# Where the feed-forward's rounded numbers become bfloat16: on VectorE, or on GpSimd behind the rounding products

## The chip, the core and the metric

The kernel runs on one core of a Trainium2 chip. A core has TensorE (PE: matrix products, written to PSUM), VectorE (DVE), ScalarE (ACT), GpSimd (POOL) and SyncE (SP), which here issues nearly all the DMA transfers. Each engine works through its own queue in order, and the engines wait for one another by semaphores. The metric is device microseconds (us) of one execution, the median of the runs. Lower is better.

## The reference, cut to what matters

The work is one decoder layer for 32 images of 256 tokens with 256 features: self-attention (16 query heads, 4 key heads), windowed cross-attention to a context (16 heads, window 64), and a gated feed-forward with 1024 inner features. Each is followed by a residual and a layer norm. The feed-forward rounds its activations to whole numbers, once ahead of the gate and up products and once ahead of the down product:

```python
def _act_quant(x):
    scale = 127.0 / jnp.clip(jnp.max(jnp.abs(x), axis=-1, keepdims=True), 1e-05)
    xq = jnp.clip(jnp.round(x * scale), -128.0, 127.0) / scale
    return x + jax.lax.stop_gradient(xq - x)

def _bitlinear(x, w):
    return jnp.einsum('bsi,oi->bso', _act_quant(x), _weight_quant(w))

gate = jax.nn.silu(_bitlinear(x, w_gate))
up = _bitlinear(x, w_up)
return _bitlinear(gate * up, w_down)
```

The rounded values are whole numbers up to 127, which bfloat16 holds exactly, so these three products run in bfloat16. All other products are float32.

## The kernel before, in words

An image's 256 tokens are two tiles of 128 partitions. The images are pipelined: while image b is in its self-attention, image b-1 is in its cross-attention and image b-2 in its feed-forward, and the projections of image b+1 are made ahead. Time is cut into slots, 16 to an image. Each part of an image is a Python generator (`self_inputs`, `cross_inputs`, `self_output`, `cross_output`, `feed_forward`) that is started in a given slot; a `yield n` in it puts what follows n slots later. The order of PE, DVE and ACT is the order in which the program is written, slot by slot. The order of POOL and of SP's queue is decided by the scheduler, from the order of the program and what each instruction waits for.

The steps that the change and the prediction touch:

- Self-attention. `project` (line 330) makes keys and queries in PSUM; DVE multiplies them with the rotary tables into `psin` and `qT` or `kT` (lines 339 and 346); `turned` (line 312) issues four DMA copies that swap the halves of psin into `other`; POOL adds that to qT or kT (line 354). Scores `s` (line 393) go through DVE (line 409, with the bias and the row's extreme) and ACT's exponential (line 427), are transposed on PE (line 471), copied by ACT (line 480) and multiplied with the values (`o`, line 492). The reciprocal sums are spread by DVE (`wide`, line 443), a DMA transpose (`planes`, line 448) and a POOL copy (`R`, line 455), and DVE multiplies o with R into `oT` (line 505). `wo` (line 513) is the output product; behind it stand the residual and statistics (lines 523, 177, 178, 528 to 531), the normalised `row` on DVE (line 538), its transposes `zqT` (line 204), and the query product `xq` of the cross-attention (line 550).
- Cross-attention. `cross_inputs` makes keys and values from the context: key statistics `rstd_zc` on POOL (lines 184 to 186), the normalised context on ACT (line 198), its transposes `zcT`, the products `xk` (line 622) and `xv` (line 634). The keys are biased on ACT (line 568), copied by two DMAs with neighbours swapped (line 573), rotated on POOL (lines 584 to 586), and copied by eight DMAs into `kTz` (line 658), one buffer for all images. The values go to `xvaug` (line 642), parts of which two DMAs copy (lines 649 and 650). `xs` (line 674) are the scores: four products at once, each on 32 rows of kTz. DVE's line 688 and ACT's line 704 follow, then transposes `xt` (line 713), ACT's copy `xpT` (line 715), and the product with the values, `xo` (line 729).
- Feed-forward. DVE finds the row's largest value and the factors (lines 790 to 799). POOL makes the rounding product (line 803): value times factor plus the constant MAGIC = 12582912 in float32, after which the sum's low bits hold the whole number. Subtracting MAGIC gives the number, written as bfloat16 into `xib` (line 805). Two DMA transposes turn xib into `xiT` (line 809), which is the stationary operand of gate and up (`ff`, line 816). After ACT's tanh (line 830) and DVE's products (lines 831 and 837), the same is done per tile with 1024 columns: largest value (line 843), factors (lines 845 to 850), POOL's rounding product (line 852), the subtraction into `hib` (line 855), a DMA transpose into `hiT` (line 857), the down product `ffo` (line 863), and residual and statistics (lines 867, 177, 178). `out_dram` is written by SP (line 194), and the next image's transposed tokens `xT` are loaded by SP (line 111).

In the kernel before, both subtractions are DVE instructions, written one slot behind the POOL product that they need.

Of the kernel before, what the change touches and what calls it, by code (L numbers as in the profile page):

```python
# [10 lines left out]
BF16 = mybir.dt.bfloat16  # L11
# [3 lines left out]
ALU = mybir.AluOpType  # L15
AX = mybir.AxisListType

P = 128
L = 256
NT = L // P  # L20
# [14 lines left out]
INNER = 1024  # L35
# [3 lines left out]
MAGIC = 12582912.0  # L39
# [12 lines left out]
def kernel(  # L52
# [27 lines left out]
    nc = tc.nc  # L80
# [5 lines left out]
    def ctile(shape, dtype, name):  # L86
        return const.tile(shape, dtype, name=name, tag=name)
# [3 lines left out]
    def bank(name, shape=(P, 512), dtype=F32):  # L91
        return ps.tile(list(shape), dtype, tag="b", name=name)
# [10 lines left out]
    def work(name, shape, bufs=2, dtype=F32):  # L103
        return sb.tile(list(shape), dtype, tag=name, name=name, bufs=bufs)

    def small(name, n):
        return sb.tile([P, 8], F32, tag="small", name=name, bufs=48)[:, 0:n]
# [47 lines left out]
    for i in range(2):  # L155


        t = ctile([P, (NT + 1) * XH * XE + 32 - XE], F32, f"xvaug{i}")
# [14 lines left out]
    def stats(src, name):  # L173

        st = small("st", 6)
        mv = small(f"mv_{name}", 2)
        nc.vector.bn_stats(st, src)
        nc.vector.bn_aggr(mv, st)
        return mv

    def rstd_of(mv, name):

        rb = small(f"rstd_{name}", 2)
        nc.gpsimd.tensor_scalar(rb[:, 0:1], mv[:, 1:2], EPS, None, ALU.add)
        nc.gpsimd.tensor_tensor(rb[:, 0:1], rb[:, 0:1], neg_half[:, 0:1], ALU.pow)
        nc.gpsimd.tensor_scalar(rb[:, 1:2], mv[:, 0:1], rb[:, 0:1], -1.0, ALU.mult, ALU.mult)
        return rb
# [598 lines left out]
    def feed_forward(b):  # L786
        x2 = state[b]["x2"]

        s = small("ffs", NT)
        nc.vector.tensor_reduce(s, x2, AX.X, ALU.max, apply_absolute_value=True)  # L790
        nc.vector.tensor_scalar(s, s, QUANT_MIN, None, ALU.max)
        up = small("ffup", NT)
        nc.vector.reciprocal(up, s)
        nc.vector.tensor_scalar(up, up, 127.0, None, ALU.mult)
        g_of = small("ffg", NT)
        nc.vector.tensor_scalar(g_of, s, ff_scale["gate"], 0.5, ALU.mult, ALU.mult)
        u_of = small("ffu", NT)
        nc.vector.tensor_scalar(u_of, s, ff_scale["up"], None, ALU.mult)
        nc.vector.tensor_tensor(u_of, u_of, g_of, ALU.mult)
        xi = work("tr", [P, NT, D], 3)  # L800
        xib = work("xib", [P, NT, D], 1, BF16)
        for t in range(NT):
            nc.gpsimd.tensor_scalar(xi[:, t, :], x2[:, t, :], up[:, t : t + 1], MAGIC, ALU.mult, ALU.add)
        yield
        nc.vector.tensor_scalar(xib, xi, MAGIC, None, ALU.subtract)  # L805

        xiT = work("xiT", [P, NT, NDC, P], 1, BF16)
        for t in range(NT):
            nc.sync.dma_start_transpose(xiT[:, t, :, :], xib[:, t, :])
        yield 3  # L810
        gu = work("gu", [P, NT, INNER], 1)

        def hidden(name, t, half):
            pg = bank("ff")
            for dc in range(NDC):
                nc.tensor.matmul(  # L816
                    pg,
                    xiT[:, t, dc, :],
                    ff_w[name][:, dc, half * 512 : (half + 1) * 512],
                    start=(dc == 0),  # L820
                    stop=(dc == NDC - 1),
                )
            return pg


        for t in range(NT):
            for half in range(2):
                pg = hidden("gate", t, half)
                cols = gu[:, t, half * 512 : (half + 1) * 512]
                nc.scalar.activation(cols, pg, AF.Tanh, scale=g_of[:, t : t + 1])  # L830
                nc.vector.scalar_tensor_tensor(cols, cols, 1.0, pg, ALU.add, ALU.mult)  # L831
            yield 1 if t == 0 else 3
        for t in range(NT):
            for half in range(2):
                pg = hidden("up", t, half)
                cols = gu[:, t, half * 512 : (half + 1) * 512]
                nc.vector.tensor_tensor(cols, cols, pg, ALU.mult)
            yield 1 + t
        d_ofs, hiTs = [], []
        for t in range(NT):  # L840

            m = small("ffm", 1)
            nc.vector.tensor_reduce(m, gu[:, t, :], AX.X, ALU.max, apply_absolute_value=True)
            sh = small("ffsh", 1)
            nc.vector.tensor_scalar(sh, m, u_of[:, t : t + 1], QUANT_MIN, ALU.mult, ALU.max)
            hup = small("ffhup", 1)
            nc.vector.reciprocal(hup, sh)
            nc.vector.tensor_scalar(hup, hup, u_of[:, t : t + 1], 127.0, ALU.mult, ALU.mult)
            d_of = small("ffd", 1)
            nc.vector.tensor_scalar(d_of, sh, ff_scale["down"], None, ALU.mult)  # L850
            d_ofs.append(d_of)
            nc.gpsimd.tensor_scalar(gu[:, t, :], gu[:, t, :], hup, MAGIC, ALU.mult, ALU.add)
            yield
            hib = work("hib", [P, INNER], 2, BF16)
            nc.vector.tensor_scalar(hib, gu[:, t, :], MAGIC, None, ALU.subtract)
            hiT = work("hiT", [P, NIC, P], 2, BF16)
            nc.sync.dma_start_transpose(hiT, hib)
            hiTs.append(hiT)
        yield 2
        for t in range(NT):  # L860
            py = bank("ffo")
            for ic in range(NIC):
                nc.tensor.matmul(  # L863
                    py[:, 0:D], hiTs[t][:, ic, :], ff_w["down"][:, ic, :], start=(ic == 0), stop=(ic == NIC - 1)
                )
            y = x2[:, t, :]
            nc.vector.scalar_tensor_tensor(y, py[:, 0:D], d_ofs[t], y, ALU.mult, ALU.add)
            mv = stats(y, "y")
            rstd = rstd_of(mv, "y")
            yield  # L870
            last.append(partial(scaled, y, y, rstd))
        last.append(partial(nc.sync.dma_start, out[b].rearrange("(t p) d -> p t d", p=P), x2))
        del state[b]
# [16 lines left out]
    for b in range(B):  # L890
        s0 = 16 * b
        if b:
            at(s0 - 15, self_inputs(b))
        at(s0 + 2, cross_inputs(b))
        for t in range(NT):
            at(s0 + 9 + 8 * t, self_output(b, t))
            at(s0 + 4 * CROSS + 11 + 8 * t, cross_output(b, t))
        at(s0 + 4 * CROSS + 26, feed_forward(b))
# [154 lines left out]
```

## Time and profile before

| | |
|---|---|
| median of 3 runs | 2186.22 us (2183.72 to 2188.77) |
| span of the profiled execution, first to last instruction | 2184.1 us |
| time of that execution beside its span | none is recorded; its span lies 2.1 us under the median |
| busy: PE | 2096.9 us (96%) |
| busy: DVE | 1778.0 us (81%) |
| busy: ACT | 1600.0 us (73%) |
| busy: POOL | 1285.1 us (59%) |
| mean granted PE clock | 0.983 |
| DMA | 177.57 MB, mean 81 GB/s |

The profile is one execution. Busy time is the time in which an engine has an instruction in work; matrix products are pipelined and their ends are modelled. A row of the groups gives line, engine, operation, the tiles written and read, shapes and count, then the busy time in us and the mean of one in ns, then the idle time of the engine just ahead of these instructions and what ended it. A row of the timeline gives start and length in us, engine, line, operation and tiles; what stands in brackets is the idle time ahead of it and its releaser. "SPq" rows are SP issuing DMAs; the transfer lands later.

### The profile page before, as it was taken

The numbers are of one execution on the slowest core, as the hardware profiler recorded it, in microseconds if no ns is written. First come the engines' busy times: TensorE is split into PE (matmuls) and PEld (weight loads), VectorE is DVE, ScalarE is ACT, GpSimd is POOL, SyncE is SP. The second block draws the span as 40 slices with busy tenths as digits, with TensorE's granted clock in tenths as the row PEclk, the third lists the DMA queues.
The fourth block names the chain that finished last, engine by engine and source line by source line (L and its number), as shares of the span: only waits on it lengthen the run. The fifth ranks groups of instructions, "written<-read, shape, count | busy, mean of one in ns | idle before, by whom it ended". The sixth has DMA issues, their size and how long they took to land.

```text
span 2184.1 us, 54367 instructions
## 1 busy us (share of the span) xinstructions
PE 2096.9 (96%) x17316; PEld 1606.7 (74%) x17316; DVE 1778.0 (81%) x6949; ACT 1600.0 (73%) x4833; POOL 1285.1 (59%) x1977
## 2 busy tenths in 40 slices
PE   7899999999999999999999999999999999999983
PEld 5677777777777777777777777777777777777751
DVE  4777888888888888888888888888888888888765
ACT  2478778777778877777877777877777877777862
POOL 4555665566655656655656655656666566666542
PEclk9899999999999999999999999999999999999986
DMA  7432333333333334334334333333343333333211
GB/s 219 111 75 72 82 75 83 77 79 86 89 72 78 83 71 91 86 71 86 76 76 89 82 77 79 78 81 83 86 82 76 81 82 74 90 81 69 53 42 32
DMA packets 326589, 177.57 MB, mean 81 GB/s; under 512 B 242976, under 2 KB 296096, under 8 KB 326304
## 3 DMA queue, kind: packets, MB, share of 16 engines
q1 hardware_dynamic: 324608, 170.52, 34.6%
q8 instruction: 139, 2.28, 0.5%
q10 hardware_dynamic: 1696, 3.57, 0.5%
q14 instruction: 146, 1.20, 0.2%
HBM read 39.50 MB, written 8.39 MB: 22 GB/s over the span
## 4 chain that ended last, share of the span: by engine, by line
PE 74%; DVE 11%; ACT 5%; POOL 4%; DMA 4%; issue 1%; SPq 0%; ACTq 0%; POOLq 0%; DVEq 0%
PE wo L513 10%; PE o L492 8%; PE proj L330 8%; PE t L471 8%; PE s L393 8%; PE ff L816 5%; PE xt L713 4%; PE xo L729 3%; PE xq L550 3%; PE xs L674 3%; PE ffo L863 3%; PE xk L622 3%; DVE p L409 2%; PE xw L775 2%; PE v L362 2%; DVE xib L805 2%
## 5 line engine op out<-in xcount | busy, mean ns | idle before, releaser
L427 ACT ACTIVATE p<-p,nm 128x256 f32<-128x256 f32 x1024 | 511.6, 512 | 197.7 <-DVE nm L409 197.7
L409 DVE CUSTOM_DVE_ANT_0 p<-s,alibi 128x256 f32<-128x256 f32 x1024 | 364.6, 416 | 6.3 <-PE s L393 6.3
L480 ACT COPY pT<-t 128x512 f32<-128x512 f32 x512 | 276.1, 601 | 89.6 <-PE t L471 89.3
L704 ACT ACTIVATE xp<-xp,xnm 128x128 f32<-128x128 f32 x1024 | 331.8, 416 | 0.0
L688 DVE CUSTOM_DVE_ANT_0 xp<-xs,mask 128x128 f32<-128x128 f32 x1024 | 225.9, 285 | 68.1 <-PE xs L674 68.1
L455 POOL COPY R<-planes 128x1024 uint16<-128x1024 uint16 x128 | 175.4, 1370 | 176.3 <-DMA planes<-wide 164.6
L471 PE MATMUL t<-ident,p 128*128 128x128 f32 x2048 | 266.4, 273 | 0.9 <-ACT p L427 0.9
L492 PE MATMUL o<-pT,v 128*64 128x256 f32 x2048 | 260.8, 386 | 1.3 <-ACT pT L480 1.1
L393 PE MATMUL s<-kT,qT 64*128 64x256 f32 x2048 | 255.7, 389 | 0.0
L513 PE MATMUL wo<-wo_sb,oT 128*128 128x256 f32 x1024 | 248.0, 386 | 0.4 <-ACT xpT L715 0.3
L354 POOL TENSOR_TENSOR qT<-qT,other 128x512 f32<-128x512 f32 x128 | 169.4, 1323 | 127.6 <-DMA other<-psin 66.4
L330 PE MATMUL proj<-xT,wq_sb 128*128 128x256 f32 x1024 | 243.1, 381 | 0.0
L471 PEld LDWEIGHTS t<-ident,p 128*128 128x128 f32 x2048 | 234.2, 141 | 9.4 <-ACT p L427 2.6
L393 PEld LDWEIGHTS s<-kT,qT 64*128 64x128 f32 x2048 | 187.3, 186 | 63.4 <-issue 14.3
L492 PEld LDWEIGHTS o<-pT,v 128*64 128x64 f32 x2048 | 143.9, 136 | 104.4 <-issue 21.2
L513 PEld LDWEIGHTS wo<-wo_sb,oT 128*128 128x128 f32 x1024 | 194.9, 193 | 30.9 <-ACT xpT L715 1.1
L427 ACT ACTIVATION_READ_ACCUMULATOR p<-p,nm 128x1 f32 x1024 | 208.0, 203 | 0.0
L330 PEld LDWEIGHTS proj<-xT,wq_sb 128*128 128x128 f32 x1024 | 185.8, 191 | 21.1 <-issue 0.4
L831 DVE SCALAR_TENSOR_TENSOR gu<-gu,ff 128x512 f32<-128x512 f32 x128 | 82.6, 684 | 84.5 <-ACT gu L830 84.3
L713 PEld LDWEIGHTS xt<-ident,xp 128*128 128x128 f32 x1024 | 110.6, 141 | 53.7 <-issue 38.5
L713 PE MATMUL xt<-ident,xp 128*128 128x128 f32 x1024 | 143.3, 281 | 2.1 <-ACT xp L704 2.0
L339 DVE TENSOR_TENSOR psin<-proj,rs_sb 128x512 f32<-128x512 f32 x160 | 109.8, 686 | 38.2 <-PE proj L330 34.6
(146 smaller groups left out, 4325.7 us busy)
## 6 DMA issues: line engine op xcount, KB each, us to landing
other<-psin SPq DMA_DIRECT2D x640, 64.0 KB, 2.0
xT<-in_xt_dram SPq DMA_DIRECT2D x32, 256.0 KB, 2.8
xs<-in_x_dram SPq DMA_DIRECT2D x32, 256.0 KB, 2.8
cs<-in_ctx_dram SPq DMA_DIRECT2D x32, 256.0 KB, 2.8
other<-qb SPq DMA_DIRECT2D x64, 128.0 KB, 2.1
kTz<-tr SPq DMA_DIRECT2D x256, 32.0 KB, 2.0
other<-qb SPq DMA_DIRECT2D x128, 64.0 KB, 2.0
out_dram<-x SPq DMA_DIRECT2D x32, 256.0 KB, 2.3
```

The lines of the kernel that those rows point to most:

```text
L330: nc.tensor.matmul(pq[:, c * L : (c + 1) * L], w[:, dc, c * P : (c + 1) * P], xT[:, dc, :], start=(dc == 0), stop=(dc == NDC - 1),)
L393: nc.tensor.matmul(banks[half][:, rr * L : (rr + 1) * L], qT[rows_, rr, qc * P : (qc + 1) * P], kT[rows_, kc, :], start=(rr == 0), stop=(r ...
L409: nc.vector.tensor_tensor_reduce(p[:, cols], banks[half][:, cols], alibi[:, 2 * (4 * kc + 2 * rp + rr) + half, :], -0.125, 3.0e38, ALU.add ...
L427: nc.scalar.activation(p[:, cols], p[:, cols], AF.Exp, bias=nm[:, rr : rr + 1], scale=-1.0, accum_out=s["sums", i // 2][:, e : e + 1],)
L455: nc.gpsimd.tensor_copy(R.bitcast(U16).rearrange("p (n z) -> p z n", z=2), s.pop(("planes", m)).rearrange("p z r q -> p z (r q)"),)
L471: nc.tensor.transpose(pt[:, j * P : (j + 1) * P], p[half][:, rr * L + kk * P : rr * L + (kk + 1) * P], ident,)
L480: nc.scalar.copy(pT, pt)
L492: nc.tensor.matmul(po[half * HD : (half + 1) * HD, rp * L : (rp + 1) * L], s["v"][:, kk, (2 * kc + half) * HD : (2 * kc + half + 1) * HD], ...
L513: nc.tensor.matmul(py[:, 0:D], s["oT", qc, kc][:, r, :], wo_sb[:, 4 * kc + r, :], start=(kc == 0 and r == 0), stop=(kc == 1 and r == 3),)
L688: nc.vector.tensor_tensor_reduce(p[:, cols], banks[2 * half + j // 2][:, j % 2 * P : (j % 2 + 1) * P], s["mask"][:, qc, :], -1.0, 3.0e38, ...
L704: nc.scalar.activation(p[:, cols], p[:, cols], AF.Exp, bias=s["xnm", i][half][:, j : j + 1], scale=-1.0)
L713: nc.tensor.transpose(pt[:, j * P : (j + 1) * P], p[:, j * P : (j + 1) * P], ident)
```

## The change

The two subtractions of MAGIC move from DVE to POOL, each behind its rounding product and ahead of the `yield`. The first one becomes two instructions of 256 columns in place of one of 512. Nothing else is written differently.

```diff
         for t in range(NT):
             nc.gpsimd.tensor_scalar(xi[:, t, :], x2[:, t, :], up[:, t : t + 1], MAGIC, ALU.mult, ALU.add)
+        for t in range(NT):
+            nc.gpsimd.tensor_scalar(xib[:, t, :], xi[:, t, :], MAGIC, None, ALU.subtract)
         yield
-        nc.vector.tensor_scalar(xib, xi, MAGIC, None, ALU.subtract)
 
         xiT = work("xiT", [P, NT, NDC, P], 1, BF16)
...
             nc.gpsimd.tensor_scalar(gu[:, t, :], gu[:, t, :], hup, MAGIC, ALU.mult, ALU.add)
+            hib = work("hib", [P, INNER], 2, BF16)
+            nc.gpsimd.tensor_scalar(hib, gu[:, t, :], MAGIC, None, ALU.subtract)
             yield
-            hib = work("hib", [P, INNER], 2, BF16)
-            nc.vector.tensor_scalar(hib, gu[:, t, :], MAGIC, None, ALU.subtract)
             hiT = work("hiT", [P, NIC, P], 2, BF16)
             nc.sync.dma_start_transpose(hiT, hib)
```

## The prediction

> **What bounds the kernel now.** I read the page's busy shares and its chain first. About 0.2% is what a measurement of this kernel can tell from no change; that is 4.4 us.
>
> ```profile
> PE 2096.9 (96%) x17316; PEld 1606.7 (74%) x17316; DVE 1778.0 (81%) x6949; ACT 1600.0 (73%) x4833; POOL 1285.1 (59%) x1977
> ...
> PE 74%; DVE 11%; ACT 5%; POOL 4%; DMA 4%; issue 1%; SPq 0%; ACTq 0%; POOLq 0%; DVEq 0%
> ```
>
> TensorE is the bound: in the stretch view PE is busy 1783.9 of the 1800 us from 130 to 1930, in steady state, where an image takes some 64.7 us. Freeing DVE is worth only the little that PE waits for DVE. Next, the groups of DVE and of POOL with shapes kept apart: the two moved conversions, and the POOL rows nearest to their new form.
>
> ```profile
> L855 DVE TENSOR_SCALAR hib<-gu 128x1024 bf16<-128x1024 f32 x64 | 58.1, 908 | 8.9 <-POOL gu L852 8.9
> ...
> L805 DVE TENSOR_SCALAR xib<-tr 128x512 bf16<-128x512 f32 x32 | 44.3, 1384 | 8.3 <-POOL tr L803 7.5
> ```
>
> ```profile
> L852 POOL TENSOR_SCALAR gu<-gu,ffhup 128x1024 f32<-128x1024 f32 x64 | 71.7, 1120 | 79.2 <-DVE ffhup L848 79.0
> ...
> L803 POOL TENSOR_SCALAR tr<-x,ffup 128x256 f32<-128x256 f32 x64 | 29.9, 480 | 0.0
> ...
> L603 POOL CAST ck_i<-ck_i 128x256 f32<-128x256 int32 x32 | 13.2, 412 | 99.1 <-DMA ck_i<-in_cell_k_dram 99.1
> ...
> L224 POOL TENSOR_SCALAR xkv_w<-tr,vecs_sb 128x256 f32<-128x256 f32 x4 | 3.7, 932 | 12.0 <-DMA tr<-in_wxk_dram 11.6 <-DMA tr<-in_wxv_dram 0.3
> ```
>
> Then the timeline around one xib in mid-run (others repeat it).
>
> ```profile
> 975.65 0.93 POOL L803 TENSOR_SCALAR tr<-x,ffup 128x256 f32<-128x256 f32 x2
> ...
> 976.61 1.49 DVE L805 TENSOR_SCALAR xib<-tr 128x512 bf16<-128x512 f32 x1 [0.42 <-POOL tr L803]
> ...
> 979.06 0.51 ACT L427 ACTIVATE p<-p,nm 128x256 f32<-128x256 f32 x1 [3.69 <-DVE nm L409]
> ...
> 980.48 0.41 PE L204 MATMUL zqT<-ident,row 128*128 128x128 f32 x2 [0.25 <-DVE row L538]
> ...
> 983.63 0.91 PE L729 MATMUL xo<-xpT,xvaug 128*32 128x64 f32 x32 [0.39 <-ACT xpT L715]
> ```
>
> Here is the one place in an image where DVE holds up PE: DVE waits 0.42 for POOL, is busy 1.49 with xib, starts its scores late, ACT its exponentials, and PE waits 0.25 and 0.39; that xo run takes 0.91 where other xo runs of 32 take 0.65. Last, SP's queue after it, and PE's first matmuls of the next image's cross-attention.
>
> ```profile
> 974.71 3.41 SPq L312 DMA_DIRECT2D other<-psin  x4
> 978.21 0.54 SPq L649 DMA_DIRECT2D xvaug<-xvaug  x1
> 978.85 0.54 SPq L650 DMA_DIRECT2D xvaug<-xvaug  x1
> 979.48 2.49 SPq L809 DMA_TRANSPOSE xiT<-xib  x2
> 982.07 0.54 SPq L194 DMA_DIRECT2D out_dram<-x  x1
> 982.70 0.41 SPq L111 DMA_DIRECT2D xT<-in_xt_dram  x1
> 983.41 2.47 SPq L312 DMA_DIRECT2D other<-psin  x4
> ...
> 989.32 5.58 SPq L658 DMA_DIRECT2D kTz<-tr  x7
> ```
>
> ```profile
> 997.34 0.50 PE L674 MATMUL xs<-kTz,xqT 32*128 32x256 f32 x4
> ```
>
> SP issues without a pause from 974.7 to 994.9, and at its end stand the kTz copies, which xs at 997.34 needs. The last kTz copy is issued at 994.3 and the page gives 2.0 us from issue to landing: 996.3, 1.05 before xs. Read so in 26 images, it lands 0.04 to 1.92 us before xs, on average 0.98. This margin decides the forecast.
>
> **The change part by part.** In the instruction order of the changed program against that of before, PE, ACT and the rest of DVE keep their order. On DVE 96 instructions go. On POOL each conversion comes behind its rounding product. On SP the xiT transposes move ahead of the projection's four psin copies and the two xvaug copies; the first hiT transpose moves ahead of one planes transpose and one of a pair of query copies.
>
> *xib off DVE.* 32 x 1.38 = 44 us of DVE time, and its wait. DVE would go from its xvaug additions (end 976.2) straight on instead of at 978.0, so some 1.8 us earlier; the scores it needs start on PE at 975.33. ACT follows by the same, and PE's waits go: 0.25 + 0.39 + (0.91 - 0.65) = 0.9 per image. The value matmuls at 991.47 take 2.33 against 1.88 to 1.95 elsewhere, behind an ACT queue that has no gap since 979: up to 0.38 more. So 0.9 to 1.3 per image, over 29 images 26 to 37 us, if nothing else comes late.
>
> A rule speaks against the move: the Trainium skill, GPSIMD Engine Reference, section 4.1, keeps elementwise work on VectorE and calls GpSimd roughly line-rate for one input. By its 1.2 GHz that is an estimated 0.85 us for 1024 elements where this trace's POOL row has 1.12 and DVE's own best is 0.68. Section 1 of that page also says that GpSimd shares its SBUF port with VectorE instructions in a two-port mode. The trace agrees: xib took 426 to 1493 ns, median 1482, with POOL at work beside it. By the page's view of DVE alone 0.43 would leave DVE's queue per image; by the row 1.48.
>
> *xib on POOL.* 64 instructions of 128x256. No row has this form; 0.41 (the cast) and 0.93 (L224, in the start-up) bound it. I take 0.48, the row L803, same engine, shape and input. The first half is ready at 976.58 + 0.48 = 977.1, the second at 977.5, earlier than DVE's 978.1. POOL's queue behind it (the key rotation, rstd_zo, two qT additions, mask) moves by 0.96. The key rotation's result is copied first at 986.0 and is ready by 980.2; rstd_zo is used at 985.2 and ready by 981.4: hidden. Cover lost costs at most 0.96 per image.
>
> *xiT ahead on SP.* This is where the change bites. SP now waits for POOL's 977.1 before it may issue the psin copies that it issued at 974.7. From the durations shown: xiT 977.1 to 979.6; psin 2.46 (3.41 in this image, 2.46 when undisturbed) to 982.1; xvaug 2 x 0.64 to 983.4; out 0.6 to 984.0; xT 0.5 to 984.5; next psin at 984.5 instead of 983.41, when DVE's psin was ready. That is 1.1 late, and all behind it is contiguous up to the kTz copies. In addition, SP's occasional longer issues in the first psin group (2.46 to 3.60, mean 2.75 in 26 images) were absorbed by the slack ahead of 983.41 and now pass on: 0.29 on average. kTz lands 1.39 later. Against the mean margin of 0.98, xs starts 0.41 later than before; the 0.9 to 1.3 that PE had won is spent waiting. With 29 images in the steady run that is +12 us. The psin copies' reader, POOL's addition at 980.5, comes to about 984; its result is needed at 1004: hidden.
>
> *hib on POOL.* 64 x 0.908 = 58 us off DVE, 64 x 1.12 onto POOL (nearest row L852, one operand less; 0.68 by DVE's best below, 1.37 by POOL's copy L455 above). In steady state PE does not wait here: the ffo matmuls read hiT over 4 us after the issue of its first transpose. Behind the second hib, R comes 1.5 later (957.6, used at 960.6) and the second key statistic 0.6 later (959.5, used by ACT at 959.2): 0.3 on ACT, whose context the transposes of zcT need at 962.0. I cost it at nothing; without that cover it would be 0.3 x 29 = 9 us.
>
> *The drain.* At 2166.7 to 2172.4 nothing hides hib. Today the second reduction waits behind the first hib on DVE (gu at 2166.74, hib at 2167.89, second hiT at 2172.42). With DVE free, the second reduction starts at 2166.8, its scale is ready at 2168.7, POOL is free of hib 1 at 2169.1, gu 2 ends 2170.2 and hib 2 at 2171.4: the second hiT 1.0 sooner. The same at 2142.3 to 2146.1: -2 us together, -1 more for the image before.
>
> **Sum.** 2184.1 (span) + 12 - 3 = 2193.1. The page has no separate time for that execution; its span lies 2.1 under the median of the timed runs, 2186.2, so the time is 2195.
>
> **The rivals.** *SP catches up; faster.* PE keeps its 0.9 to 1.3 per image where kTz lands before xs is ready for it, at 996.0 to 996.4 in the image shown; from a kTz delay under 0.98 instead of 1.39 on, the sign turns. SP's long issues decide: they take 1.0 on average between the first psin and the last kTz copy, and the shifted stream may place them elsewhere. For it: an image of before without them lands kTz at 18.8 after xib, here 995.4, and 1.1 later is 996.5. Against: nearly every image has one. Price: from half of the 26 upward, with the drain's -3, but short of the whole 37: -12 to -34, so 2152 to 2174. *POOL's conversion is dear.* At 0.93 the first half comes 0.45 later, so does kTz: 29 x 0.45 = 13 more, and hib at 1.4 adds little: about 2208; a form as slow as POOL's mask compare (1239 ns for 128 elements) would be +60. *Nothing.* PE bound, gain and loss equal: 2184 to 2190. That the move is not made is excluded by the order.
>
> **How the numbers follow.** The kTz wait decides 0.55, with +3 to +17 (2189 to 2203); SP catches up 0.25; dear conversion 0.10; nothing 0.10. Range 2166 to 2212: it leaves out the full gain and the slow form. Faster takes 0.25 + 0.02 of the edge of nothing, same 0.08 + 0.09 of the first case's edge, slower the rest, 0.56.
>
> **What would show it.** Right: DVE's scores at the xib place some 1.8 us earlier, PE's waits before zqT and xo there gone, psin issued behind xiT, and a new PE wait at xs for the kTz transfer of 1 us or more. Wrong: xs without a wait (then PE's image is 0.9 to 1.3 shorter), POOL's xib far from 0.48, or a wait of ACT for rstd_zc.

## The result: 3.7% slower

The changed kernel takes 2265.1 us (2258.2 to 2276.8, six runs) against 2188.4 (2183.7 to 2189.1, six runs) of the kernel before: a ratio of 1.037 with an interval of 1.035 to 1.039. The forecast was 2195 with a range to 2212: right in sign, 70 us short in size, and beyond the end of its range.

### The profile page after: what moved, and what is told of

Same layout as the page of the kernel before. It is cut to its first block, busy times and chain, and to the rows that moved or that the text cites. A ratio compares the mean times of both kernels' runs of the same rounds, so it can differ in the third digit from the quotient of the medians.

```text
span 2256.4 us, 54367 instructions
## 1 busy us (share of the span) xinstructions
PE 2124.4 (94%) x17254; PEld 1626.7 (72%) x17316; DVE 1743.5 (77%) x6853; ACT 1608.0 (71%) x4833; POOL 1502.0 (67%) x2105
## 4 chain that ended last, share of the span: by engine, by line
PE 68%; DVE 9%; POOL 9%; DMA 4%; ACT 4%; issue 4%; SPq 2%; ACTq 0%; POOLq 0%; DVEq 0%
PE wo L513 9%; PE proj L330 8%; PE o L492 8%; PE s L393 8%; PE t L471 7%; PE ff L817 4%; PE xt L713 4%; PE xs L674 4%; POOL hib L855 3%; PE xo L729 3%; PE xk L622 2%; DMA kTz<-tr 2%; PE xv L634 2%; SPq L658 2%; PE xq L550 2%
## 5 line engine op out<-in xcount | busy, mean ns | idle before, releaser
L513 PE MATMUL wo<-wo_sb,oT 128*128 128x256 f32 x1024 | 254.3, 393 | 17.3 <-ACT xpT L715 17.3
L354 POOL TENSOR_TENSOR qT<-qT,other 128x512 f32<-128x512 f32 x128 | 163.7, 1279 | 117.3 <-DMA other<-psin 68.9
L513 PEld LDWEIGHTS wo<-wo_sb,oT 128*128 128x128 f32 x1024 | 199.6, 198 | 56.7 <-ACT xpT L715 24.0
L855 POOL TENSOR_SCALAR hib<-gu 128x1024 bf16<-128x1024 f32 x64 | 178.4, 2788 | 5.5
L674 PE MATMUL xs<-kTz,xqT 32*64 32x256 f32 (+1 forms) x1536 | 117.7, 410 | 35.5 <-POOL xqT L586 18.2
```

The lines of the kernel that those rows point to most:

```text
L513: nc.tensor.matmul(py[:, 0:D], s["oT", qc, kc][:, r, :], wo_sb[:, 4 * kc + r, :], start=(kc == 0 and r == 0), stop=(kc == 1 and r == 3),)
L674: nc.tensor.matmul(banks[r][:, 0 : 2 * P].rearrange("p (h k) -> p h k", k=P)[q0:q1], s["xqT", qc][rows_, ch, q0:q1], kTz[rows_, ch, :, k0 ...
L855: nc.gpsimd.tensor_scalar(hib, gu[:, t, :], MAGIC, None, ALU.subtract)
```

## The profile after

First the busy line and the chain's shares by engine:

```profile
PE 2124.4 (94%) x17254; PEld 1626.7 (72%) x17316; DVE 1743.5 (77%) x6853; ACT 1608.0 (71%) x4833; POOL 1502.0 (67%) x2105
...
PE 68%; DVE 9%; POOL 9%; DMA 4%; ACT 4%; issue 4%; SPq 2%; ACTq 0%; POOLq 0%; DVEq 0%
```

POOL's work grew by 217 us, where 102 (58.1 + 44.3) were taken off DVE; DVE's own fell by only 34 (the last section says why). PE's share of the chain fell from 74% to 68% and POOL's rose from 4% to 9%. Now the groups of POOL with shapes kept apart: the two new rows, the two rows that had priced them, and one from the start-up.

```profile
L855 POOL TENSOR_SCALAR hib<-gu 128x1024 bf16<-128x1024 f32 x64 | 178.4, 2788 | 5.5
...
L853 POOL TENSOR_SCALAR gu<-gu,ffhup 128x1024 f32<-128x1024 f32 x64 | 71.9, 1124 | 68.4 <-DVE ffhup L849 68.1
...
L805 POOL TENSOR_SCALAR xib<-tr 128x256 bf16<-128x256 f32 x64 | 54.5, 867 | 0.0
...
L803 POOL TENSOR_SCALAR tr<-x,ffup 128x256 f32<-128x256 f32 x64 | 30.1, 483 | 0.0
...
L224 POOL TENSOR_SCALAR xkv_w<-tr,vecs_sb 128x256 f32<-128x256 f32 x4 | 3.7, 935 | 11.8 <-DMA tr<-in_wxk_dram 11.4 <-DMA tr<-in_wxv_dram 0.3
```

The number ahead of the second bar is the mean in ns. xib takes 867 where L803 was to price it (483), hib 2788 where L853 was (1124). The start-up's L224 takes 935 at xib's shape. The timeline around one xib, and PE behind it:

```profile
1006.41 1.70 POOL L805 TENSOR_SCALAR xib<-tr 128x256 bf16<-128x256 f32 x2
...
1009.32 0.38 PE L204 MATMUL zqT<-ident,row 128*128 128x128 f32 x2
...
1011.98 0.65 PE L729 MATMUL xo<-xpT,xvaug 128*32 128x64 f32 x32
```

No bracket stands behind zqT and xo now: the waits of 0.25 and 0.39 are gone, and the xo run takes 0.65. What that cost is in SP's queue and at the next image's first scores:

```profile
1007.31 2.46 SPq L810 DMA_TRANSPOSE xiT<-xib  x2
1009.86 2.46 SPq L312 DMA_DIRECT2D other<-psin  x4
...
1015.07 2.46 SPq L312 DMA_DIRECT2D other<-psin  x4
...
1021.69 4.70 SPq L658 DMA_DIRECT2D kTz<-tr  x7
```

```profile
1022.97 1.34 POOL L455 COPY R<-planes 128x1024 uint16<-128x1024 uint16 x1 [2.10 <-DMA planes<-wide]
...
1025.73 0.72 POOL L586 TENSOR_TENSOR xqT<-qb,other 128x256 f32<-128x256 f32 x1
...
1026.51 0.90 PE L674 MATMUL xs<-kTz,xqT 32*128 32x256 f32 x6 [1.22 <-POOL xqT L586]
...
1027.91 0.67 PE L674 MATMUL xs<-kTz,xqT 32*128 32x256 f32 x2 [0.51 <-DMA kTz<-tr]
...
1029.10 1.55 PE L817 MATMUL ff<-ff_up,xiT 128*128 128x512 bf16 x3
...
1030.44 1.91 PE L513 MATMUL wo<-wo_sb,oT 128*128 128x256 f32 x4
```

xiT stands ahead of the psin copies, and SP issues without a gap to the end of kTz. (The rows left out are the xvaug copies, the store and the load, and behind the second psin group the first kTz copy, two query copies and a planes transpose, as before.) xs waits twice, for its rotated queries and for kTz. Both come out of SP's queue: POOL turns the queries behind its copy R, which waited 2.10 for the planes transpose. The same two PE stages in the kernel before:

```profile
998.57 1.04 PE L816 MATMUL ff<-ff_up,xiT 128*128 128x512 bf16 x4
999.45 1.89 PE L513 MATMUL wo<-wo_sb,oT 128*128 128x256 f32 x8
```

Behind the two waits PE itself ran slower: four products of wo took the time of eight. The granted PE clock was 0.5 there, for 3.41 us from 1029.5 on. In the 1800 us from 130 on, the changed kernel has nine such stretches, each behind waits at xs, and the kernel before has none; at half the clock they cost an estimated 9 x 1.7 = 15 us.

Last, from the list of waits (total us, times, longest us), the waits at xs and the other new wait; before, these rows had 10.4, 4.4, 0.3 and 0.2 us:

```profile
ACT cs L198 <- POOL rstd_zc L186: 84.2, 60, 3.1
...
PE xs L674 <- POOL xqT L586: 18.2, 21, 2.4
...
PE wo L513 <- ACT xpT L715: 17.3, 28, 1.0
...
PE xs L674 <- DMA kTz<-tr: 16.2, 29, 0.7
```

ACT's wait comes from the place of hib on POOL, between the steps of an image's first key statistic and ahead of its second; the wait of wo follows behind ACT's copies xpT:

```profile
982.42 0.22 POOL L184 TENSOR_SCALAR rstd_zc<-mv_zc 128x1 f32<-128x1 f32 x1
...
982.73 2.79 POOL L855 TENSOR_SCALAR hib<-gu 128x1024 bf16<-128x1024 f32 x1
...
985.48 0.57 POOL L185 TENSOR_TENSOR rstd_zc<-rstd_zc,neg_half 128x1 f32<-128x1 f32 x1
...
988.04 0.60 ACT L198 ACTIVATE cs<-cs,rstd_zc 128x256 f32<-128x256 f32 x1 [1.60 <-POOL rstd_zc L186]
...
989.50 0.60 ACT L198 ACTIVATE cs<-cs,rstd_zc 128x256 f32<-128x256 f32 x1 [0.86 <-POOL rstd_zc L186]
...
991.61 1.13 PE L513 MATMUL wo<-wo_sb,oT 128*128 128x256 f32 x4 [0.43 <-ACT xpT L715]
```

Where the loss sits is read from the starts of PE's stages, in 28 images of the steady run, by subtracting each kernel's mean distance from one stage to the next:

| PE's stage (us per image, against before) | after |
|---|---|
| waits for DVE at zqT, xo, s and o, gone | -1.09 |
| next image's first cross scores: into xs 0.58, xs to xo 1.46, and xo to t behind them 0.55 (there the clock fell) | +2.59 |
| zcT to wo (ACT late behind the key statistics), and xs behind it | +0.94 |
| image period (64.81 before, 67.24 after) | +2.42 |

The 28 periods are 68 us, and the drain takes 5.0 more (from PE's last `xv` to the end 116.4 against 111.4); the spans of the two profiled executions differ by 72.3.

## The experiments

Theory T, formed from these rows: POOL's conversions are 1.8 and 2.5 times as dear as priced, and two separate mechanisms charge for it, SP's queue (xib) and a late key statistic (hib; the expectations call it the second, by the rows above both are late). Rival R1: POOL's sum of load. R2: not SP's order but POOL's own lateness holds xs. R3: DVE is slowed by POOL beside it. In all experiments the kernel before had medians of 2185.1 to 2187.5 us.

### One conversion at a time

The first kernel takes only the xib part of the diff, the second only the hib part.

> Only the first conversion (xib, 64 instructions of 128x256 on POOL); hib stays on DVE. Theory T, two separate losses: the changed kernel's per-image sum is -1.09 (waits of PE for DVE gone) + 2.6 (first cross scores of the next image held by the kTz copies) + 0.94 (zcT and wo held behind ACT's wait for the second key statistic) = +2.45 us; here the 0.94 should go, so about +1.5 x 29 = +44: 2232 us, POOL's xib at 0.87 us and xs still waiting for the kTz transfer by 1 us or more per image. Rival R1 (POOL's total load is what hurts, each part alone is harmless): within 10 us of the kernel before. Rival R3 (DVE is slowed by POOL's conversions and that is the loss): DVE's wide copy near 709 ns again, and a loss under half of the full change's 79 us.

Measured: 2216.9 us, ratio 1.014 (1.012 to 1.016).

> Only the second conversion (hib, 64 instructions of 128x1024 on POOL); xib stays on DVE. Theory T: POOL's hib at 2.79 us keeps the second key statistic and R late, ACT waits for it, zcT and wo come late by 0.94 us an image: 2186 + 0.94 x 29 = about 2214 us, with no wait of xs for the kTz transfer beyond that of before (0.65 us in the xs to xo step). R1 (only the sum of both loads hurts): within 10 us of before. R3 (contention on DVE): DVE's wide copy near 1007 ns as in the full change and the loss at PE's waits for DVE, not for ACT.

Measured: 2231.8 us, ratio 1.021 (1.019 to 1.022). The two losses, 1.4% and 2.1%, add up to 3.5%, against 3.7% together, so R1 falls. By PE's stages they are disjoint: xib alone has -1.1 at the waits for DVE and +2.38 at the first cross scores, nothing at zcT; hib alone has +1.13 from zcT over wo to xs, +0.16 at zqT, and nothing at the first cross scores. T had 2232 and 2214: xib costs less (its drain is 4.2 us shorter than before, 107.2), hib more, of which 8.8 us are the drain (120.2 from the last `xv` to the end). In the 1800 us from 130 on the clock fell to 0.5 ten times with xib alone and once with hib alone. The waits of the second kernel:

```profile
ACT cs L198 <- POOL rstd_zc L186: 82.4, 60, 3.2
...
PE wo L513 <- ACT xpT L715: 19.5, 28, 1.0
```

R3 has something for it, but not at the place of the loss. DVE's copy `wide` (line 443) takes 709 ns before, 777 with xib moved, 934 with hib moved, 1007 with both. With xib moved, PE's waits for DVE nevertheless fell; with hib alone they rose by the 0.16 at zqT. The new ones name kTz, xqT and ACT. That hib holds ACT through the key statistics is read from the rows and these waits; no run changed POOL's order alone.

### SP's queue made shorter

One query projection of each image leaves out the four psin copies that stand ahead of kTz; that part of the rotation is computed with the unswapped values.

```diff
-            other = turned(psin.rearrange("p c t -> p (c t)"))
+            flat = psin.rearrange("p c t -> p (c t)")
+            other = turned(flat) if swap else flat
...
-            pair = project(wq_sb[:, :, j * 2 * P : (j + 1) * 2 * P], 0)
+            pair = project(wq_sb[:, :, j * 2 * P : (j + 1) * 2 * P], 0, swap=j != 2)
```

On the changed kernel:

> The full change, but one of the query projections of each image leaves out the four copies of psin that swap its halves (that part of the rotation is computed with the unswapped values). SP's queue is 2.46 us shorter ahead of the kTz copies and nothing else is meant to change. Theory T (SP's order puts kTz late): the wait of xs for kTz goes, PE's first cross scores come 2 us or more sooner, and the time falls to about 2265 - 2.4 x 29 = 2195 us; what is left is ACT's wait for the second key statistic. Rival R2 (POOL's own lateness, the rotation or the query additions, holds xs): xs still waits, for xqT from POOL instead of kTz, and the time stays within 15 us of 2265.

On the kernel before:

> The kernel before, with the four psin copies of one query projection left out (that part of the rotation is computed with the unswapped values), as in the kernel that fell from 2265 to 2188.5. Theory T (before, kTz lands 0.98 us ahead of xs, so a shorter SP queue gains nothing): 2180 to 2190 us. Rival R2 (the omission saves POOL and DMA work that is worth as much in any kernel): 70 us below before.

Measured: 2188.5 on the changed kernel (1.0007 of before, 0.9997 to 1.0016), 2183.4 on the kernel before (0.9988, 0.9979 to 0.9998). Four copies fewer ahead of kTz are worth 77 us in the one and 2 us in the other. Of the stages, +0.07 is left at the first cross scores, +1.11 from zcT to xs, and the -1.10 stays. So R2 falls: it is SP's queue that held xs. With the wait the lower clock went too: one stretch in the 1800 us in place of nine. The omission also spares POOL's addition its wait for these copies, which this pair can't set apart from SP's issuing.

### The price of POOL's forms

A kernel of its own measured forms of `tensor_scalar` on POOL, at first to ask whether the bfloat16 output was dear.

> A measurement by itself, which computes nothing of the reference: POOL's forms one after the other, four or more of each, and DVE's conversion alone, beside POOL additions and beside POOL conversions. Theory T1 (the bfloat16 output makes POOL's form dear): multiply-and-add with a pointer from float32 to float32 at 1.1 us for 1024 elements, subtract to float32 near it, both to bfloat16 near 2.8, the plain copy to bfloat16 dear too. Rival T2 (the subtract by a constant without a second operation is dear, not the type): subtract to float32 near 2.8 too, multiply-and-add to bfloat16 near 1.1. Rival T3 (POOL was slowed by DVE beside it): subtract to bfloat16 alone at 1.1 to 1.5 here, and 256 elements at 0.4 to 0.5. DVE's 512-element conversion: 0.43 us alone, 1.0 us or more beside POOL.

Its groups (L29 is multiply by a pointer and add, to float32; L35 the same to bfloat16; L31 and L33 subtract one constant, to float32 and to bfloat16; L59 and L66 are DVE's conversion of 512 columns, beside POOL's two-input additions and, as the timeline shows, with POOL idle):

```profile
L33 POOL TENSOR_SCALAR half<-src 128x1024 bf16<-128x1024 f32 x4 | 11.1, 2768 | 0.0
L31 POOL TENSOR_SCALAR wide<-src 128x1024 f32<-128x1024 f32 x4 | 11.1, 2768 | 0.0
L59 DVE TENSOR_SCALAR d<-src 128x512 bf16<-128x512 f32 x10 | 10.2, 1018 | 0.3
...
L29 POOL TENSOR_SCALAR wide<-src,sc 128x1024 f32<-128x1024 f32 x4 | 4.5, 1118 | 0.5 <-DMA src<-in_x_dram 0.5
L35 POOL TENSOR_SCALAR half<-src,sc 128x1024 bf16<-128x1024 f32 x4 | 4.5, 1118 | 0.0
...
L66 DVE TENSOR_SCALAR d<-src 128x512 bf16<-128x512 f32 x10 | 4.3, 426 | 0.3
```

T1 and T3 fall: the output's type changes nothing, and POOL alone is as slow (256 columns took 0.84 to 0.85 us with DVE idle, and up to 1.62 beside DVE's conversions). T2 stands in part: subtracting one constant is the dear form. A plain copy to bfloat16 took 1.04 us. Whether it is the operation, the missing second operation or the operand was asked twice more:

> A measurement by itself, which computes nothing of the reference: POOL alone, forms of a scalar operation over 128x1024 float32 to bfloat16, two of each. The first such measurement had 2.77 us for one subtract of a constant, to float32 as to bfloat16, and 1.12 us for a multiply by a pointer and an add, to either. Theory U1 (one operation without a second is the slow form, whatever the operation): subtract, add, multiply alone near 2.8 us each, with a pointer or a constant; every pair of operations near 1.1. Rival U2 (subtract is slow): add alone and multiply alone near 1.1, and both pairs with a subtract near 2.8. Rival U3 (a pointer is fast, a constant slow): pairs with constants near 2.8, multiply alone by a pointer near 1.1.

Measured, in us for 1024 elements: subtract alone 2.91, add alone 2.77, multiply alone 2.77 with a constant and 2.84 with a pointer; subtract and add of constants 3.63; multiply and subtract 3.63; multiply by a pointer and add 1.12. U1 holds for one operation, but not for pairs.

> A measurement by itself, which computes nothing of the reference: POOL alone, 128x1024 float32 to bfloat16, two of each pair of operations, to find what of the fast form makes it fast. So far multiply by a pointer and add a constant took 1.12 us, one operation 2.8, and subtract-add and multiply-subtract by constants 3.7. Theory W1 (only the pair multiply, add is fast, whatever the operands): multiply and add by constants near 1.1, multiply by a pointer and subtract 3.7. Rival W2 (a pointer as the first operand of any pair is fast): multiply and add by constants 3.7, multiply by a pointer and subtract, multiply by it twice, and add by it near 1.1.

(The lines of this kernel: L38 multiply and add by constants, L42 by two pointers, L44 multiply twice, L40 multiply and subtract, L46 add twice, L48 add alone.)

```profile
L40 POOL TENSOR_SCALAR half<-src,one 128x1024 bf16<-128x1024 f32 x2 | 7.4, 3714 | 0.2
L46 POOL TENSOR_SCALAR half<-src,one 128x1024 bf16<-128x1024 f32 x2 | 7.4, 3712 | 0.2
L48 POOL TENSOR_SCALAR half<-src,one 128x1024 bf16<-128x1024 f32 x2 | 5.7, 2848 | 0.2
...
L42 POOL TENSOR_SCALAR half<-src,one 128x1024 bf16<-128x1024 f32 x2 | 2.4, 1193 | 0.2
L44 POOL TENSOR_SCALAR half<-src,one 128x1024 bf16<-128x1024 f32 x2 | 2.2, 1118 | 0.2
L38 POOL TENSOR_SCALAR half<-src 128x1024 bf16<-128x1024 f32 x2 | 2.1, 1047 | 0.2
```

It is the pair of operations, not the operand: multiply followed by add or by multiply takes 1.05 to 1.19, every other form tried 2.8 (one operation) or 3.7 (two). (The first instruction of each of these two kernels took longer than its twin: L36 here, multiply by a pointer and add, 1.65 and then 1.12; the single subtract 3.05 and then 2.77.) W1 is right on add and missed the multiply pair; W2 is wrong on constants, on subtract and on add twice.

### The change at other prices

Before the second of these measurements was known, I took two operations of any kind for the fast form. That guess was wrong, and it became an experiment on a dearer POOL.

```diff
-MAGIC, None, ALU.subtract)
+MAGIC, 0.0, ALU.subtract, ALU.add)
```

Both conversions:

> The full change with both conversions as two operations in one instruction (subtract the constant, add 0.0) in place of one. If that form takes 0.48 us (xib) and 1.12 us (hib), this is the kernel that the prediction's sum was made for. Theory T (the sum's prices failed, and with the right ones its steps hold): POOL's xib near 0.48, hib near 1.12; SP's first transpose 0.39 us sooner than in the changed kernel, kTz 0.39 sooner, ACT's wait for the second key statistic nearly gone: 2190 to 2215 us. Rival V (the places, not the prices, did the harm): 2235 us or more even at those prices. Rival U2 (subtract is slow in any form): 2265 again, with xib near 0.87.

Only hib:

> Only hib on POOL, as two operations in one instruction; xib on DVE. The same with one operation took 2231.8, 44 us over before. Theory T: hib near 1.12 us, ACT's wait for the second key statistic falls from 82 us to 10 to 20 in all, 2180 to 2197 us. Rival V (the order on POOL, hib ahead of the statistic and the key rotation's copies, does the harm at any price): 2215 or more.

Measured: 2297.6 us for both (1.050, 1.046 to 1.054), 2256.4 for hib alone (1.033, 1.030 to 1.035), with xib at 1.10 us and hib at 3.66. The times rise with the price: hib alone costs 1.33 us an image at 2.79 and 1.94 at 3.66. The expectations had the price wrong, so neither T nor V could be told by these, but they bear on R3: in the second kernel the copy `wide` took 740 ns, near the 709 of before, and hib cost more than as a single subtract, beside which that copy took 934. So it is not this hold on DVE that charges for hib. The next kernel tells T from V, with the form that the measurement had shown to be fast:

```diff
-MAGIC, None, ALU.subtract)
+ones[:, 0:1], -MAGIC, ALU.mult, ALU.add)
```

> The full change with both conversions as a multiply by a column of ones and an add of minus the constant, the one form that took 1.12 us for 1024 elements on POOL. This is the kernel that the prediction's sum was made for. Theory T (prices failed; with the right ones the steps hold, but the wait of xs also costs what follows it): xib near 0.48, hib near 1.12, first transpose on SP 0.36 us sooner than with xib alone moved at 0.87 (0.86 after the rounding product there), kTz 0.36 sooner, hib's loss 0 to 0.2 an image: 2200 to 2218 us. The prediction's own sum, without any follow-on cost: 2195. Rival V (the places on POOL and SP do all the harm): 2240 or more.

Measured: 2186.6 us against 2185.1 before, ratio 0.9999 (0.998 to 1.002). Its groups and waits:

```profile
L855 POOL TENSOR_SCALAR hib<-gu,ones 128x1024 bf16<-128x1024 f32 x64 | 71.6, 1119 | 5.9
...
L805 POOL TENSOR_SCALAR xib<-tr,ones 128x256 bf16<-128x256 f32 x64 | 29.9, 480 | 0.0
```

```profile
ACT cs L198 <- POOL rstd_zc L186: 32.8, 42, 3.4
...
PE xs L674 <- DMA kTz<-tr: 12.0, 22, 0.7
```

With the same places and the same order, the loss of 77 us is gone by the form of two instructions alone; V falls. These are the very prices of the sum, 0.48 and 1.12, and PE's period is 0.24 longer than before: -1.10 at the waits for DVE, +1.36 at the first cross scores, nothing at zcT. PE's last stretch is 5.2 us shorter (106.2). The time fell below both expectations: T's cost behind xs hardly shows at this price (0.06 an image; the clock fell in one image).

How kTz comes late, as means over 26 images, in us from the end of POOL's rounding product:

| | first xiT issue | first psin issue behind it | next psin group | last kTz landed |
|---|---|---|---|---|
| before | 2.32 | -1.82 (ahead of xiT) | 6.88 | 19.78 |
| fast form, both | 0.48 | 3.05 | 8.37 | 21.04 |
| xib alone, as changed | 0.86 | 3.43 | 8.93 | 21.49 |
| fast form, shorter SP queue (below) | 0.48 | 3.04 | 7.12 | 19.92 |

### Towards a better kernel

If DVE's waits come from the place of xib in its queue, xib could stay on DVE one turn later:

```diff
-        yield
+        yield 2
         nc.vector.tensor_scalar(xib, xi, MAGIC, None, ALU.subtract)
...
-        yield 3
+        yield 2
```

> The kernel before with xib still on DVE, but taken one turn later in the order that is written out, so that DVE's scores stand ahead of it and SP's transposes of xib stand behind the xvaug copies. Theory (PE's waits of 0.9 to 1.1 us an image come from xib standing ahead of the scores in DVE's queue, and SP's late kTz is what the move to POOL cost): those waits go, kTz lands as before or up to 1 us later, and the time falls by 0.5 to 1 x 29: 2158 to 2172 us. Rival (any xib that comes later pushes SP's kTz copies past xs): within 10 us of before or slower, with PE's xs waiting for the kTz transfer.

Measured: 2203.8 us, ratio 1.008 (1.006 to 1.010). The rival was right: the waits for DVE went here too (-0.66 an image at zqT, xo and xq, -0.20 at s and o), but xiT was issued from 5.5 to 8.0, the next psin group at 8.85 in place of 6.88, kTz landed at 21.33, and the first cross scores and what follows gave back 1.70. So DVE need not lose the conversion to lose the stall, and SP's queue decides in either case.

Then the two DMAs that stand in that queue without hurry, the store of the output and the load of xT, were given to POOL to issue:

```diff
-        nc.sync.dma_start(xT, xt[b])
+        (nc.gpsimd if b else nc.sync).dma_start(xT, xt[b])
...
-        last.append(partial(nc.sync.dma_start, out[b]
+        last.append(partial(nc.gpsimd.dma_start, out[b]
```

With xib on POOL in the fast form, hib on DVE:

> xib on POOL in the multiply-and-add form, hib on DVE, and the two DMAs of each image that stand between the xvaug copies and the next psin copies on SP (the store of the output, the load of xT) issued by POOL instead: SP is 1.1 us shorter ahead of kTz. Theory T: kTz lands about 0.2 us later than before, inside the margin of 0.98, and PE keeps the 1.09 us an image that it gains: 2155 to 2168 us. Rival: POOL's queue pays for the two issues (each over 1 us there, or waiting for the output's last scaling) and its additions and key rotation come late: 2187 or more.

With both conversions on POOL in the fast form:

> Both conversions on POOL as multiply and add, and the output's store and xT's load issued by POOL. Alone, the form made 2187 (no change) and, with hib on DVE, the two issues made 2161. Theory T (hib at 1.12 us costs PE nothing, and frees the drain by 3 us): 2152 to 2163 us. Rival (hib ahead of the second key statistic costs some once the kTz wait no longer covers it): 2168 to 2180, with ACT's wait for that statistic above 30 us in all.

With the kernel before:

> The kernel before, with only the store of the output and the load of xT issued by POOL instead of SP. Theory T (before, kTz has a margin, so a shorter SP queue is worth nothing there; the gain of 24 us needs both edits): 2178 to 2190 us. Rival (the issues were the whole gain and the move of xib none): 2155 to 2168.

Measured: 2161.1 us (0.9895, 0.988 to 0.991), 2161.3 (0.989, 0.987 to 0.990), and 2185.8 (1.0002, 0.999 to 1.002). The queue alone is worth nothing, both fast conversions alone nothing, all together 1.1% (xib alone in the fast form, with SP's queue as before, was not run). With the queue as before, the late kTz takes back what the move wins; with xib on DVE, kTz was not what PE waited for. The second kernel's ACT still waits 33.9 us in all for the key statistic, so hib moved gains nothing but costs nothing. In the first kernel the next psin group goes out at 7.12 and kTz lands at 19.92 (the table's last row), 0.14 later than before.

What is left is 0.41 us an image from xs to xo. Two of the eight kTz copies were given to POOL as well:

```diff
-                nc.sync.dma_start(kTz[rows_, :, j, :], kT[rows_, :, :])
+                (nc.gpsimd if r == 3 else nc.sync).dma_start(kTz[rows_, :, j, :], kT[rows_, :, :])
```

> xib on POOL as multiply and add, hib on DVE, store and xT load issued by POOL (2161 so far), and two of the eight kTz copies of an image issued by POOL as well. Theory T (what is left at the first cross scores, 0.41 us an image, is still the kTz copies on SP): kTz ready 1 us or more sooner, 2161 - 0.41 x 29 = about 2149, 2145 to 2156. Rival (POOL reaches those two issues too late, or the wait left is for xqT or DVE): 2158 to 2175.

Measured: 2172.5 us (0.994, 0.993 to 0.996), slower than without. xs now waits for POOL's rotated queries (15.9 us in 22 waits of PE against 5.6 in 5): by these waits POOL pays for the issues, as the rival said.

## Why the prediction was wrong

**The step that failed is the price of POOL's conversions.** xib was taken at 0.48 us a half and measured 0.87, hib at 1.12 and measured 2.79. The rows were chosen by engine, shape and type; what decides is the form, one operation or a pair that begins with a multiply. The right row was in the profile and in the text: L224, one operation over 128x256, 0.93, set aside as an upper bound from the start-up. A second one-operation row, L234 (604 ns for 128 columns), gives with it (932 - 604) / 128 = 2.56 ns an element, and 0.93 + 768 x 0.00256 = 2.9 us for hib, where the bounds given were 0.68 to 1.37. The bounds for hib were taken from DVE and from a copy, and not from the form that bounded xib. Two of the signs that were named for being wrong came true: xib far from 0.48, and ACT's wait for rstd_zc.

**A rule and the rows.** The Trainium skill, GPSIMD Engine Reference, section 4.1, calls GpSimd roughly line-rate for one input; the runs agree for a copy (1.04 us for 1024 elements) and for multiply and add (1.12), and do not for a single subtract, add or multiply (2.8). Its advice against elementwise work on GpSimd held for the kernel as changed.

**With the price right, the steps held.** DVE's waits: 0.9 to 1.3 us an image forecast, 1.09 measured. kTz later: 1.39 forecast, 1.26 measured in the fast form (21.04 against 19.78). Net at xs: +0.41 forecast, +0.24 measured. hib, put at nothing: nothing measured at 1.12, with ACT's wait for the statistic up from 10.4 to 32.8 us as the text feared. The drain: -3 forecast, -5.2 measured. The sum of 2195 was made for these prices, and they gave 2186.6; of the 8 us between, 29 x 0.17 = 5 are at xs and 2 in the drain.

**The rival of dear conversions had the right cause and the wrong size.** It gave 13 us to 0.93 and "adds little" to hib. From 0.48 to 0.87, kTz lands 0.45 later (0.45 was the forecast for 0.93), but PE's period grows by 1.01 (1.25 with xib alone at 0.87, 0.24 in the fast form with hib): 0.30 more into xs, where PE's wait for xqT rose from 5.6 to 14.4 us in all, since POOL turns it behind R, which waits for a transpose in the same queue; 0.20 from xs to xo; and the rest at ff, wo and t behind it. For this last part the sum had no term, and the traces show what it is: the granted PE clock fell to 0.5 for 3.41 us ten times with xib alone and once in the fast form, an estimated 9 x 1.7 / 28 = 0.55 an image. What decides it stays open: in the changed kernel the clock fell behind waits at xs of 0.99 to 1.73 us in all, and did not fall behind others of up to 1.98. And hib at 2.79 was no small matter: it stands between the steps of the first key statistic and ahead of the second on POOL, so ACT waits, its copies xpT behind that come late, and wo waits for them: 1.33 us an image, and 8.8 in the drain.

**Nothing** was not the likeliest case, yet the fast form landed on it, by the luck of two sizes: mechanisms of 1.1 and 1.4 us an image almost cancel, and one cheaper queue turns the balance.

## What to carry to other kernels

Price an operation on POOL by its form as well as its shape: look for a row with the same number and kind of operations, in the start-up too, and write a subtraction of a constant there as a multiply by one and an add. Where a profile shows an engine's stall next to an in-order DMA queue without gaps, count that queue first: here removing the stall paid only when the queue was shortened too. A queue that is worth nothing to shorten by itself may be what a second edit needs.

## What the runs showed of the hardware

POOL's `tensor_scalar` has three prices by form: 1.05 to 1.19 us for multiply-add and multiply-multiply over 128x1024 (the first instruction of a kernel aside), 2.77 to 2.91 for one operation, 3.63 to 3.71 for multiply-subtract, subtract-add and add-add, the same for a float32 and a bfloat16 output in both forms that were run with each. DVE's conversion of 512 columns took 426 ns with POOL idle and 1018 beside POOL's two-input additions; beside POOL's single-operation conversions, four conversions of 1024 columns took 866 each, about twice 426, so the slow form held these conversions up little. It did hold DVE's copies of line 443, which is why DVE got less than it was relieved of: in the changed kernel 29 of them ran beside hib and took 1.47 us on the average, against 0.69 with POOL idle, and 55 ran beside the two-input additions of lines 354 and 540 and took 1.01. Beside hib as subtract and add, 29 took 0.70. The mean of all went from 709 ns to 1007, 38 us in all, and to 720 with the fast form. The granted PE clock, 1.00 throughout the steady run of before, fell to 0.5 for 3.41 us at a time behind some of the short waits of PE: none, one, nine, ten and twenty times in the 1800 us from 130 on in the kernel before, the fast form, the changed kernel, xib alone, and both conversions as subtract and add.
